# Graph attention's last row tiles: sums and bias on VectorE, a last step for what the keys don't need, and four buffers for the keys' halves

## The chip, the cores and the metric

The kernel runs on one core of one Trainium2 chip. The metric is the device time of one execution in microseconds; lower is better. Times are medians of several runs. A profile is one execution, with every instruction's start and length in a trace.

The engines are named as the profile names them: PE (TensorE's matmuls), PEld (its weight loads), DVE (VectorE), ACT (ScalarE), POOL (GpSimd) and SP, which only issues DMAs. A DMA can be issued on SP's or on POOL's queue; each engine and each queue works through its instructions in the order in which they stand there.

## What is computed

Two layers work on 2708 nodes with 512 features. Each normalizes its input, clears what is negative, and adds its result to its input. The first is a graph attention of eight heads; the second builds an attention of its own from the features and diffuses over it in two steps. Cut to what matters here:

```python
# layer 0: graph attention, H = 8 heads of D = 64
h = jnp.maximum(_layernorm(x, axis=-1), 0.0)
feats = jnp.einsum('nf,hfd->hnd', h, W)
dense = leaky_relu(e_self[:, :, None] + e_neigh[:, None, :]) + mask[None, :, :]
out = jnp.einsum('hnm,hmd->hnd', softmax(dense), feats) + b[:, None, :]
x = x + relu(out)                               # heads side by side
# layer 1: its input is the normalized, cleared x of layer 0
v = jnp.maximum(_layernorm(x, axis=-1), 0.0)
for s in range(2):
    Q, K = Xa @ W1, Xa @ W3                     # Xa starts as v
    A = nucleus_softmax(Q @ W2 @ K.T)           # keeps 0.9 of each row's mass
    Xf, Xb, Xa = Rf @ Xf, Rb @ Xb, A @ Xa
    Z = Z + (Xf @ U1[s] + Xb @ U2[s] + Xa @ U3[s])
x = x + layernorm(v + Z) * gamma + beta
```

## The kernel before

The nodes are cut into 22 row tiles, 21 of 128 rows and a last one of 20.

**The first layer** goes through six chunks of columns; the first four have four tiles, the last two three. The last chunk holds tiles 19, 20 and 21, which is 276 columns. For each chunk and each group of four heads a loop over all 22 tiles forms the attention's weights on DVE (L427) and multiplies them on PE (L429). ACT then copies the sums to `o_t` (L434). What turns a chunk's sums into finished rows is `finished`, for one tile at a time, in five steps:

- `turned`: loads the tile's x (`xt`) and transposes the sums on PE (L351).
- `shared`: the denominators and their reciprocal (L360, L362) and the sum for rows without neighbours (L365) on DVE; then on POOL the multiplication by the reciprocal (L367) and the bias of the attention (L368).
- `normed`: relu and the addition of x on DVE (L372); `moments`, which is two steps on DVE (L137, L138) and two on POOL (L139, L140); then on POOL the second layer's `beta` added into `xt` (L374) and its DMA to `xb_d` (L375).
- `cleared`: the normalization on DVE (L381), the clearing on ACT (L382), which gives `v`, and its DMA to `va_d` on POOL's queue (L383).
- `asked`: transposes v on PE (L389) and copies it on ACT (L391). `split_rows` splits v into a high and a low half: zeros into a ragged tile (L180, POOL), the high half (L181, DVE), the low half (L182, here on POOL) and a DMA of 512 KB to `vhl_d` (L183, POOL's queue). `project` forms keys and queries on PE (L160), takes them over on ACT (L165, L166), splits them on POOL (L170 to L172; L164 writes zeros first for the ragged tile) and sends them to `kq_d` (L173, POOL's queue).

In the first five chunks the steps of a finished chunk are spread over the next chunk's loop. For the last chunk (`final`) there is no such loop: `later` is filled by step, and each step is issued for the three tiles before the next step begins. The buffers of `split_rows` and `project` come from the pool `halves`, with one buffer per name. The order of the instructions on each engine in the first layer is made by a planner. It starts from the order of the code and from what is ready by its own estimate of times, and so it can differ from the code's order.

**The second layer** does two steps with the order on PE, ACT, DVE and SP fixed by the code. Its first instructions load the keys of all tiles from `kq_d` (L930: tiles 0 to 19 in a first pair of DMAs, tiles 20 and 21 in a second), then the queries (L509); then PE forms the logits of the first pair of tiles (L521), which ACT copies (L523) and DVE reduces (L548). `split_rows` and `project` are called there too, with pools of their own. `vhl_d` is read by L961, one row tile after the other, along with `s_d` (L963) for the diffusion's products on PE (L967); `va_d` by L937; `xb_d` at the end of the last step.

Of the kernel before, what the change touches and what calls it, by code (L numbers as in the profile page):

```python
# [9 lines left out]
F32 = mybir.dt.float32  # L10
# [14 lines left out]
P = 128  # L25
# [28 lines left out]
def kernel(  # L54
# [19 lines left out]
    nc = tc.nc  # L74
    N, D = x.shape
    H, _, DH = w_gat.shape
# [12 lines left out]
    TG = 4  # L89
# [42 lines left out]
    def moments(pool, src, pr):  # L132

        st = pool.tile([P, 6], F32, name="ln_st")
        mv = pool.tile([P, 2], F32, name="ln_mv")
        rs = pool.tile([P, 1], F32, name="ln_rs")
        nc.vector.bn_stats(st[:pr], src)  # L137
        nc.vector.bn_aggr(mv[:pr], st[:pr])  # L138
        nc.gpsimd.tensor_scalar(rs[:pr], mv[:pr, 1:2], LN_EPS, None, op0=OP.add)  # L139
        nc.gpsimd.tensor_tensor(rs[:pr], rs[:pr], nhalf[:pr], OP.pow)  # L140
        return mv[:pr, 0:1], rs[:pr]
# [10 lines left out]

    kw = const.tile([P, KD, 2 * DA], F32, name="kw")

    def project(pool, pk, v_t, t, s):


        pr = rows[t]
        for k in range(KD):
            nc.tensor.matmul(pk[:, :pr], lhsT=kw[:, k, :], rhs=v_t[:, k, :pr], start=(k == 0), stop=(k == KD - 1))  # L160
        big = pool.tile([P, P], F32, name="kq_b")
        hl = pool.tile([P, 2, P], F32, name="kq_hl")
        if pr < P:
            nc.gpsimd.memset(hl, 0.0)  # L164
        nc.scalar.copy(hl[:, 1, :pr], pk[:, :pr])  # L165
        nc.scalar.mul(big[:, :pr], pk[:, :pr], 4097.0)  # L166


        high, x = hl[:, 0, :pr], hl[:, 1, :pr]
        nc.gpsimd.tensor_tensor(high, big[:, :pr], x, op=OP.subtract)  # L170
        nc.gpsimd.tensor_tensor(high, big[:, :pr], high, op=OP.subtract)
        nc.gpsimd.tensor_tensor(x, x, high, op=OP.subtract)  # L172
        nc.gpsimd.dma_start(out=kq_d[s][:, :, t * P:(t + 1) * P], in_=hl)  # L173
# [28 lines left out]
    with ExitStack() as l0:  # L202
# [13 lines left out]
        with tc.tile_pool(name="l0w", bufs=1) as wp, tc.tile_pool(name="l0p", bufs=2) as pp, \  # L216
# [44 lines left out]
            for t in range(NT):  # L261
                pr = rows[t]
# [70 lines left out]
                            ap=[[0, P], [N, len(grp)], [1, cw]]))  # L333
            return r_b

        def finished(t, o_t, c0, bank):


            pr = rows[t]
            f3 = fsum.rearrange("p (h d) -> p h d", h=H)  # L340
            pns, held = [], []

            def turned():
                xt = work.tile([P, D], F32, name="xt0", bufs=3)
                nc.sync.dma_start(out=xt[:pr], in_=x[cols[t], :])
                held.append(xt)
                for g, grp in enumerate(hgroups):
                    pn = bank(g)
                    pns.append(pn[:, :HG * DV].rearrange("p (h d) -> p h d", h=HG))
                    for i, hd in enumerate(grp):  # L350
                        nc.tensor.transpose(pns[g][:pr, i, :], o_t[:, hd, c0:c0 + pr], ident[:DV, :DV])  # L351

            def shared():
                den = small.tile([P, H], F32, name="den")
                rden = small.tile([P, H], F32, name="rden")
                o = work.tile([P, D], F32, name="o", bufs=3)
                held.append(o)
                o3 = o.rearrange("p (h d) -> p h d", h=H)
                for pn, grp in zip(pns, hgroups):
                    nc.vector.tensor_scalar(den[:pr, grp[0]:grp[-1] + 1], pn[:pr, :, DH],  # L360
                                            lone_n[:pr, t:t + 1], None, op0=OP.add)
                nc.vector.reciprocal(rden[:pr], den[:pr])  # L362
                for pn, grp in zip(pns, hgroups):
                    s = slice(grp[0], grp[-1] + 1)
                    nc.vector.scalar_tensor_tensor(o3[:pr, s, :], f3[:pr, s, :], lone[:pr, t:t + 1],  # L365
                                                   pn[:pr, :, :DH], op0=OP.mult, op1=OP.add)
                nc.gpsimd.tensor_mul(o3[:pr], o3[:pr], rden[:pr].unsqueeze(2).to_broadcast([pr, H, DH]))  # L367
                nc.gpsimd.tensor_add(o[:pr], o[:pr], b_b[:pr])  # L368

            def normed():  # L370
                xt, o = held
                nc.vector.scalar_tensor_tensor(o[:pr], o[:pr], 0.0, xt[:pr], op0=OP.max, op1=OP.add)  # L372
                held.extend(moments(small, o[:pr], pr))
                nc.gpsimd.tensor_add(xt[:pr], o[:pr], beta_b[:pr])  # L374
                nc.gpsimd.dma_start(out=xb_d[cols[t], :], in_=xt[:pr])  # L375

            def cleared():
                _, o, mean, rs = held
                v = work.tile([P, D], F32, name="v", bufs=3)
                held.append(v)  # L380
                nc.vector.tensor_scalar(o[:pr], o[:pr], mean, rs, op0=OP.subtract, op1=OP.mult)  # L381
                nc.scalar.activation(v[:pr], o[:pr], AF.Relu)  # L382
                nc.gpsimd.dma_start(out=va_d[cols[t], :], in_=v[:pr])  # L383

            def asked():
                v = held[4]
                pt = bank(0).rearrange("p (k d) -> p k d", k=KD)
                for k in range(KD):
                    nc.tensor.transpose(pt[:, k, :pr], v[:pr, k * P:(k + 1) * P], ident[:pr, :pr])  # L389
                v_t = work.tile([P, KD, P], F32, name="v_t", bufs=2)  # L390
                nc.scalar.copy(v_t[:, :, :pr], pt[:, :, :pr])  # L391
                split_rows(halves, nc.gpsimd, v[:pr], t, vhl_d)
                project(halves, bank(1), v_t, t, 0)

            return [turned, shared, normed, cleared, asked]

        later = {}
        for ci, tiles in enumerate(tchunks):
            n0, n1 = tiles[0] * P, min((tiles[-1] + 1) * P, N)
            cw = n1 - n0  # L400
            r_bs = [shares(grp, n0, cw) for grp in hgroups[:1]]
            a_c = []
            for t in range(NT):
                pr = rows[t]
                a_c.append(adjp.tile([P, 512], F32, name="a_c", bufs=NT + 2))
                nc.sync.dma_start(out=a_c[t][:pr, :cw], in_=adj_t[cols[t], n0:n1])
                s_c = small.tile([P, 512], F32R, name="s_c", bufs=4)
                wide = len(tiles) * P
                if pr < P or cw < wide:
                    nc.gpsimd.memset(s_c.bitcast(F32), 0.0)  # L410
                nc.scalar.activation(s_c[:pr, :cw], a_c[t][:pr, :cw], AF.Copy,  # L411
                                     accum_out=cpart[:pr, t, ci:ci + 1])
                if t in tiles:
                    d = slice(t * P - n0, t * P - n0 + pr)
                    nc.gpsimd.tensor_tensor(s_c[:pr, d], s_c[:pr, d].bitcast(F32), ident[:pr, :pr], op=OP.add)
                nc.sync.dma_start(out=s_d[t * P:(t + 1) * P, n0:n0 + wide], in_=s_c[:, :wide].bitcast(F32))
            for t in tiles:
                row_sums(t)
            r_bs += [shares(grp, n0, cw) for grp in hgroups[1:]]
            o_t = work.tile([DV, H, 512], F32, name="o_t", bufs=1)  # L420
            for grp, r_b in zip(hgroups, r_bs):
                po = [ps_o.tile([P, 512], F32, name="po")[:DV] for _ in grp]
                for t in range(NT):
                    pr = rows[t]
                    for i, hd in enumerate(grp):
                        e = tp.tile([P, 512], F32, name="e")
                        nc.vector.scalar_tensor_tensor(e[:pr, :cw], r_b[:pr, i, :cw], kk[:pr, t, hd:hd + 1],  # L427
                                                       a_c[t][:pr, :cw], op0=OP.max, op1=OP.mult)
                        nc.tensor.matmul(po[i][:, :cw], lhsT=fw[:pr, t, hd, :], rhs=e[:pr, :cw],  # L429
                                         start=(t == 0), stop=(t == NT - 1))  # L430
                    for stage in later.pop(t, ()):
                        stage()
                for i, hd in enumerate(grp):
                    nc.scalar.copy(o_t[:, hd, :cw], po[i][:, :cw])  # L434

            final = ci == len(tchunks) - 1
            for i, t in enumerate(tiles):
                if final:
                    bank = lambda g: ps_o.tile([P, 512], F32, name="po")
                else:  # L440
                    bank = lambda g: ps_t.tile([P, 512], F32, name=f"pn{g}")
                for n, stage in enumerate(finished(t, o_t, t * P - n0, bank)):
                    later.setdefault(n if final else i * 5 + n, []).append(stage)
        for n in sorted(later):
            for stage in later[n]:
# [832 lines left out]
```

## Time and profile before

| | |
|---|---|
| median of three runs | 3710.2 us (3706.47 to 3715.27) |
| profiled execution, its own time | 3708.3 us |
| span of the profiled execution | 3706.5 us |
| busy, share of the span | PE 91%, DVE 70%, PEld 47%, ACT 42%, POOL 22% |
| TensorE's clock granted, mean | 0.966 |
| last matmul of the first layer's loop ends | 1052.4 us after the span's start |
| first matmul of the second layer starts | 1098.1 us |

A line of the timeline has the start and the length in us, the engine, the line of the code, the operation, the tile written and the tiles read, the shape, how many instructions were merged and, in brackets, how long the engine stood idle before it and what released it. A line of the waits has who waited, for what, the total in us, how often and the longest. The lines themselves stand in the prediction.

### The profile page before, as it was taken

How to read it: one execution, taken by the hardware profiler on the slowest of the kernel's cores; microseconds unless marked ns; L12 is line 12 of the kernel's file. 1: busy time of each engine (PE TensorE's matmuls, PEld its weight loads, DVE VectorE, ACT ScalarE, POOL GpSimd, SP SyncE). 2: the span in 40 equal slices, each digit the busy share in tenths (PEclk: the TensorE clock that was granted, in tenths of full speed). 3: DMA queues.
4: the chain of work that ended last, by engine and by line, in shares of the span. 5: the costliest groups of instructions: out<-in, count | busy, mean ns of one | idle time of the engine just before them, and what ended most of it. 6: DMA issues, size and time to landing. Idle time of an engine off the chain costs nothing. (4 is left out here: it accounts for less than half of the span.)

```text
span 3706.5 us, 35338 instructions
## 1 busy us (share of the span) xinstructions
PE 3367.4 (91%) x11143; PEld 1754.4 (47%) x11143; DVE 2612.9 (70%) x4820; ACT 1541.5 (42%) x2334; POOL 799.6 (22%) x1119
## 2 busy tenths in 40 slices
PE   7998999998966988989899899688999999999898
PEld 4433333333444545545455453445655565556452
DVE  4588888889957637365463651969988779777991
ACT  2343212111114674655666612345654556445511
POOL 4114140514331112121202121302112111121101
PEclk9999999999978999999999999999999999999999
DMA  3477424233228445454535353966556665566552
GB/s 113 152 252 243 137 80 150 80 105 103 74 87 278 164 157 187 145 183 149 205 131 196 128 191 100 302 203 225 175 187 208 233 216 204 183 213 234 201 201 66
DMA packets 276459, 634.08 MB, mean 171 GB/s; under 512 B 37210, under 2 KB 70442, under 8 KB 273244
## 3 DMA queue, kind: packets, MB, share of 16 engines
q1 hardware_dynamic: 249183, 540.99, 44.2%
q0 software_dynamic: 27024, 90.30, 6.3%
q8 instruction: 89, 1.46, 0.2%
q14 instruction: 163, 1.33, 0.1%
HBM read 509.07 MB, written 122.10 MB: 170 GB/s over the span
## 5 line engine op out<-in xcount | busy, mean ns | idle before, releaser
L1035 PE MATMUL a<-va,at 128*128 128x512 f32 (+2 forms) x1936 | 890.1, 599 | 14.0 <-ACT at L1020 13.5
L967 PE MATMUL q<-hl,s_r 128*128 128x512 f32 x2904 | 820.9, 429 | 62.5 <-DMA s_r<-s_d 62.2
L429 PE MATMUL po<-e,fw 128*65 128x512 f32 (+4 forms) x2112 | 838.7, 552 | 34.3 <-DVE e L427 21.8
L427 DVE SCALAR_TENSOR_TENSOR e<-r_b,kk,a_c 128x512 f32<-128x512 f32 (+4 forms) x1056 | 751.8, 741 | 73.5 <-PE po L429 23.7
L967 PEld LDWEIGHTS q<-hl,s_r 128*128 128x128 f32 x2904 | 544.4, 190 | 307.5 <-issue 133.2
L553 ACT ACTIVATE junk_a<-p,nth 128x2708 uint8<-128x2708 f32 (+1 forms) x240 | 613.1, 2554 | 70.6 <-POOL nth L572 66.8
L429 PEld LDWEIGHTS po<-e,fw 128*65 128x65 f32 (+1 forms) x2112 | 286.2, 140 | 546.7 <-issue 269.2
L1035 PEld LDWEIGHTS a<-va,at 128*128 128x128 f32 (+2 forms) x1936 | 337.1, 187 | 379.4 <-issue 342.7
L1076 PE MATMUL a<-u_k,v_t 128*128 128x512 f32 (+1 forms) x1056 | 489.9, 601 | 22.3 <-ACT xa L1043 15.4
L629 DVE SCALAR_TENSOR_TENSOR junk<-p,th 128x2708 bf16<-128x2708 f32 (+1 forms) x132 | 401.2, 3039 | 4.0
L1020 ACT COPY at<-t 128x512 f32<-128x512 f32 (+3 forms) x308 | 140.4, 477 | 494.5 <-PE t L1016 494.1
L1076 PEld LDWEIGHTS a<-u_k,v_t 128*128 128x128 f32 (+1 forms) x1056 | 188.9, 187 | 242.1 <-issue 182.9
L521 PE MATMUL t<-keys,q_t 128*128 128x452 f32 x528 | 167.1, 443 | 118.4 <-ACT p L523 98.1
L181 DVE TENSOR_SCALAR split_hl<-xe 128x512 int32<-128x512 int32 (+1 forms) x44 | 19.1, 434 | 257.1 <-ACT xe L977 210.7
L808 DVE MAX8 vn<-keep 128x8 f32<-128x2708 f32 (+1 forms) x66 | 196.8, 2981 | 2.3
L523 ACT COPY p<-t 128x452 f32<-128x452 f32 (+2 forms) x264 | 132.0, 538 | 126.5 <-PE t L521 82.3
L521 PEld LDWEIGHTS t<-keys,q_t 128*128 128x128 f32 x528 | 91.7, 211 | 189.2 <-ACT p L523 150.7
L411 ACT ACTIVATE s_c<-a_c 128x512 fp32r<-128x512 f32 (+3 forms) x132 | 76.1, 577 | 247.5 <-DMA a_c<-in_adj_t_dram 120.7
L1016 PE MATMUL t<-ident,keep 128*128 128x128 f32 (+1 forms) x968 | 147.2, 274 | 27.1 <-DVE keep L757 19.2
L1016 PEld LDWEIGHTS t<-ident,keep 128*128 128x128 f32 (+1 forms) x968 | 115.0, 139 | 107.5 <-issue 79.5
L548 DVE TENSOR_REDUCE nmx<-p 128x1 f32<-128x2708 f32 (+1 forms) x44 | 129.0, 2966 | 41.7 <-ACT p L523 41.7
L565 POOL TENSOR_TENSOR x<-sums,powers 128x4 f32<-128x4 f32 x22 | 44.7, 2033 | 508.7 <-ACT p L560 508.7
(296 smaller groups left out, 3151.9 us busy)
## 6 DMA issues: line engine op xcount, KB each, us to landing
s_r<-s_d SPq DMA_DIRECT2D x330, 256.0 KB
hl<-vhl_d SPq DMA_DIRECT2D x132, 512.0 KB
u_k<-in_L_gnn_U_dram SPq DMA_DIRECT2D x264, 256.0 KB
hl<-fhl_d SPq DMA_DIRECT2D x132, 512.0 KB
hl<-bhl_d SPq DMA_DIRECT2D x132, 512.0 KB
arow<-in_adj_dram SPq DMA_DIRECT2D x21, 1354.0 KB
s_d<-s_c SPq DMA_DIRECT2D x88, 256.0 KB
a_c<-in_adj_t_dram SPq DMA_DIRECT2D x84, 256.0 KB
```

The source lines that it names most:

```text
L427: nc.vector.scalar_tensor_tensor(e[:pr, :cw], r_b[:pr, i, :cw], kk[:pr, t, hd:hd + 1], a_c[t][:pr, :cw], op0=OP.max, op1=OP.mult)
L429: nc.tensor.matmul(po[i][:, :cw], lhsT=fw[:pr, t, hd, :], rhs=e[:pr, :cw], start=(t == 0), stop=(t == NT - 1))
L521: nc.tensor.matmul(pl[:, :c1 - c0], lhsT=q[:, i], rhs=self.keys[:, c0:c1], start=(i == 0), stop=(i == 1))
L523: nc.scalar.copy(p[:pr, c0:c1], pl[:pr, :c1 - c0])
L553: nc.scalar.activation(junk[:pr], self.p[i][:pr], func, **kw)
L629: v.scalar_tensor_tensor(junk_b[:pr], ps_[i][:pr], th, ps_[i][:pr], op0=OP.is_ge, op1=OP.mult, accum_out=dst)
L808: v.max(vs, keep[0][:pr])
L967: nc.tensor.matmul(half[j], lhsT=s_r[:, j * P:(j + 1) * P], rhs=hl[:, h], start=(c == 0 and h == 0), stop=(c == NT - 1 and h == 1))
L1016: nc.tensor.transpose(pt[:rows[c], j, :pr], keep[i][:pr, cols[c]], ident[:pr, :pr])
L1020: nc.scalar.copy(at[:r, j0:j1, :pr], pt[:r, j0:j1, :pr])
L1035: nc.tensor.matmul(pa[:pr], lhsT=at[:rows[c], j, :pr], rhs=va[:rows[c], c, :], start=(c == 0), stop=(c == NT - 1))
L1076: nc.tensor.matmul(pz[i][:rows[t]], lhsT=v_t[i][:, k, :rows[t]], rhs=u_k, start=(n == 0 and k == 0), stop=(n == 2 and k == KD - 1))
```

## The change

Four things change, all for the last chunk's three tiles, but for the number of buffers, which holds for every tile of the first layer.

- `finished` is told whether the chunk is the last one (`final`). If so, L367's multiplication and L368's addition are done by DVE instead of POOL.
- In `normed`, for the last chunk, DVE copies the rows o into `xt` before the moments; the addition of beta and its DMA (L374, L375) leave this step. They become `with_beta`, which then reads the copy.
- In `asked`, for the last chunk, `split_rows` is left out. A sixth step, `rest`, is issued after all others: `split_rows`, with the low half on DVE instead of POOL, and then `with_beta`.
- `project`'s two tiles, `kq_b` and `kq_hl`, get four buffers (`TG`) in the first layer instead of one. The second layer's calls are as before.

```diff
-    def project(pool, pk, v_t, t, s):
+    def project(pool, pk, v_t, t, s, bufs=None):
...
-        big = pool.tile([P, P], F32, name="kq_b")
-        hl = pool.tile([P, 2, P], F32, name="kq_hl")
+        big = pool.tile([P, P], F32, name="kq_b", bufs=bufs)
+        hl = pool.tile([P, 2, P], F32, name="kq_hl", bufs=bufs)
...
-                nc.gpsimd.tensor_mul(o3[:pr], o3[:pr], rden[:pr].unsqueeze(2).to_broadcast([pr, H, DH]))
-                nc.gpsimd.tensor_add(o[:pr], o[:pr], b_b[:pr])
+                eng = nc.vector if final else nc.gpsimd
+                eng.tensor_mul(o3[:pr], o3[:pr], rden[:pr].unsqueeze(2).to_broadcast([pr, H, DH]))
+                eng.tensor_add(o[:pr], o[:pr], b_b[:pr])
 
             def normed():
                 xt, o = held
                 nc.vector.scalar_tensor_tensor(o[:pr], o[:pr], 0.0, xt[:pr], op0=OP.max, op1=OP.add)
+                if final:
+                    nc.vector.tensor_copy(xt[:pr], o[:pr])
                 held.extend(moments(small, o[:pr], pr))
+                if not final:
+                    with_beta(o)
+
+            def with_beta(o):
+                xt = held[0]
                 nc.gpsimd.tensor_add(xt[:pr], o[:pr], beta_b[:pr])
                 nc.gpsimd.dma_start(out=xb_d[cols[t], :], in_=xt[:pr])
...
-                split_rows(halves, nc.gpsimd, v[:pr], t, vhl_d)
-                project(halves, bank(1), v_t, t, 0)
-
-            return [turned, shared, normed, cleared, asked]
+                if not final:
+                    split_rows(halves, nc.gpsimd, v[:pr], t, vhl_d)
+                project(halves, bank(1), v_t, t, 0, bufs=TG)
+
+            def rest():
+                split_rows(halves, nc.vector, held[4][:pr], t, vhl_d)
+                with_beta(held[0])
+
+            return [turned, shared, normed, cleared, asked] + [rest] * final
...
-                for n, stage in enumerate(finished(t, o_t, t * P - n0, bank)):
+                for n, stage in enumerate(finished(t, o_t, t * P - n0, bank, final)):
```

More of the change, by code (lines that the diff above doesn't have):

```diff
@@ L334, in shares, with finished @@
             return r_b
-        def finished(t, o_t, c0, bank):
+        def finished(t, o_t, c0, bank, final):
             pr = rows[t]
```

## The prediction

> **What bounds the kernel now.** I read the page first, then busy time by stretch around the end of the first layer, then the timeline, then the waits.
>
> ```profile
> PE 3367.4 (91%) x11143; PEld 1754.4 (47%) x11143; DVE 2612.9 (70%) x4820; ACT 1541.5 (42%) x2334; POOL 799.6 (22%) x1119
> ```
>
> TensorE is busy 91% of the span. The change touches none of its large groups, so it can only pay where TensorE stands still. The busy times (length, then PE, PEld, DVE, ACT, POOL, granted clock, DMA share, GB/s):
>
> ```profile
> 1000.00:1030.00 30.00, 30.00 (x128) 16.95 (x127) 30.00 (x71) 1.54 (x4) 1.79 (x4) 1.00 0.05 17
> 1060.00:1080.00 20.00, 8.56 (x36) 7.31 (x36) 9.12 (x18) 4.05 (x10) 18.64 (x26) 0.50 0.23 90
> 1080.00:1110.00 30.00, 11.29 (x38) 7.64 (x39) 5.72 (x3) 8.58 (x16) 5.98 (x11) 0.62 0.62 188
> ```
>
> Until 1052 PE and DVE are full. Then comes a hole of some 46 us: POOL is the busy engine in its first half (18.64 of 20), and hardly any engine works in its second. The timeline (start, length, engine, line; in brackets the idle time before) says what the hole consists of:
>
> ```profile
> 1052.88 0.22 DVE L360 TENSOR_SCALAR den<-po,lone_n 128x4 f32<-128x4 f32 x1 [4.69 <-PE po L351]
> 1056.62 1.51 DVE L372 SCALAR_TENSOR_TENSOR o<-o,xt 128x512 f32<-128x512 f32 x1 [0.34 <-POOL o L368]
> 1061.88 2.93 POOL L374 TENSOR_TENSOR xt<-o,beta_b 128x512 f32<-128x512 f32 x2
> 1065.38 0.25 POOL L139 TENSOR_SCALAR ln_rs<-ln_mv 128x1 f32<-128x1 f32 x1
> 1066.81 0.55 DVE L381 TENSOR_SCALAR o<-o,ln_mv,ln_rs 128x512 f32<-128x512 f32 x1 [2.41 <-POOL ln_rs L140]
> 1077.36 1.90 PE L160 MATMUL po<-v_t,kw 128*128 128x20 f32 x8 [0.37 <-ACT v_t L391]
> 1085.17 0.94 POOL L180 MEMSET split_hl<- 128x1024 f32 x1 [3.18 <-DMA vhl_d<-split_hl]
> 1088.14 0.31 POOL L164 MEMSET kq_hl<- 128x256 f32 x1 [2.03 <-DMA kq_d<-kq_hl]
> 1088.49 0.17 ACT L165 COPY kq_hl<-po 128x20 f32<-128x20 f32 x1 [9.16 <-POOL kq_hl L164]
> 1091.40 0.69 POOL L173 DMA_DIRECT2D kq_d<-kq_hl  x1 [0.29 <-POOL kq_hl L172]
> 1094.77 5.20 SPq L509 DMA_DIRECT2D q_t<-kq_d  x8
> 1098.13 5.01 PE L521 MATMUL t<-keys,q_t 128*128 128x452 f32 x12 [18.87 <-DMA q_t<-kq_d]
> ```
>
> Four things are to be seen. First, DVE's L372 takes 1.51 us here against a median of 0.679 in the chunks before: POOL's L367 runs beside it. Second, POOL does L374 of two tiles ahead of L139, though the code issues the moments first: the planner gives an idle engine whatever is ready, and L381 of tile 19 pays for it. Third, the last matmul of the keys (tile 21, L160) ends at 1079.26, but ACT takes its result at 1088.49 only. POOL had to write zeros into the two single buffers, which waited for the DMAs of tile 20. Fourth, the keys' DMA behind SP's queue waits for the last kq_d write, and L509 and everything of the second layer stand behind it. The waits agree:
>
> ```profile
> PE t L521 <- DMA q_t<-kq_d: 18.9, 1, 18.9
> ACT kq_hl L165 <- POOL kq_hl L164: 9.2, 1, 9.2
> ```
>
> **What the Trainium skill says.** "SBUF — State Buffer", section on the two separate sides: VectorE with two SBUF inputs and GpSimd share one pair of ports, and the loser is blocked for the whole instruction. The trace agrees: 1.51 against 0.679 us. "DMA: Bandwidth & Descriptors", section "Anatomy of one DMA": about 2.0 us plus bytes over 436 GB/s for a DMA issued on GpSimd. For the 128 KB of kq_d that makes 2.3 us (measured median 2.3), for the 512 KB of vhl_d 3.2 (measured 2.9 at the least). Same page, "SWDGE vs HWDGE vs iDMA": each DMA engine takes turns between its queues. In the trace tile 20's two writes take 6.2 and 6.8 us, since the 1.3 MB of keys issued from 1078.98 move beside them.
>
> **The change, part by part.**
>
> (1) Sums and bias on VectorE. POOL loses L367 and L368 of three tiles (1.03 to 1.59 us each). DVE gains six operations of 128x512 with two SBUF sources. The same form on DVE is L182 in the second layer, 0.692 us; neighbours overlap by about 0.07 (L137 starts 0.07 before L372 ends), so a step of 0.62 and 3.7 us in all. DVE's own share before is 1052.88 to 1056.29. With the six it ends at 1060.0.
>
> (2) The copy. One fp32 copy of 128x512 per tile, which no row shows. DVE's single-source rows of that size are L181 (0.42) and L381 (0.546): I take 0.5, on DVE's path. Per tile then L372 0.68, copy 0.50, L137 0.68, L138 0.17, less four overlaps: 1.75, three tiles 5.3, to 1065.3. The bias on the last step (L374) is ready as soon as the copy is, so I expect the planner to give it to an idle POOL again; one collision with L372 costs 0.83. L381 of tile 19 thus at 1066.1 instead of 1066.81: **0.7 us** won. Bounds: 1063.3 if the planner lets it in as soon as its L140 is done, 1067.5 with two collisions and some.
>
> (3) From there to the last L160 nothing is removed: L381, L382, L389, L391 and L160 of three tiles took 1066.81 to 1079.26, 12.45 us, with TensorE at clock 0.50. The same span gives 1078.6. Lower bound: the PE work alone (1.12+2.08+1.06+2.08+0.61+1.90 = 8.85) back to back, 2.4 us earlier.
>
> (4) Four buffers for the keys' halves. L164's zeros wait for nothing and go early; L165 no longer waits for a DMA. After L160, ACT needs 0.5 (tile 19: 1072.85 to 1073.32), and L170 to L172 at the pace of tile 21 (0.32 each) with 0.3 before the DMA 1.3: L173 at 1080.4 instead of 1091.40. In the other chunks these waits don't exist (POOL's L170 waits for ACT alone), so the buffers do nothing there.
>
> (5) What the keys don't need goes last: L180 to L183, L374 and L375 of three tiles, with L182 on DVE (3 x 0.692, behind L381 on DVE where nobody on the path waits). Each is queued on POOL with L173: L374 4.5, L375 1.9, L183 1.7, L180 0.94, together 9.0 us. The path's own POOL work after 1061 is 10.9 (L139 and L140 2.5, L383 1.8, L164 0.3, L170 to L172 4.2, L173 2.1). All 20 us fit just before 1081, so the cover is thin: I charge half an L374, 0.8 us, in front of tile 21's. L173 at 1081.2. A step that waits for a DMA's landing (L180, and L183 behind DVE's L181) is worse than a long one: its price is a rival below. The bound below is nothing, if the planner lets only ready work in.
>
> (6) From L173 to L521 it took 6.73 us (1091.40 to 1098.13): landing, the keys' second DMAs, q_t. Kept: L521 at 1087.9.
>
> Sum: 1098.1 - 1087.9 = **10.2 us**. Is it kept afterwards? The second layer starts from this point with all engines idle, and its first chain (L521, ACT's copies, DVE's maximum, the search) hangs on L521 alone. The deferred writes (1.5 MB of vhl_d, 0.55 MB of xb_d) can fall into a stretch with a DMA share of 0.97 (1110 to 1150), where 1 MB at its 332 GB/s is 3 us. But TensorE's fills there are through at 1181, and its next work waits 13.3 us for ACT, so 3 us vanish in that. vhl_d's last rows are read last, xb_d in the last step.
>
> The profiled execution took 3708.3 us (span 3706.5), which makes 3698.1; the median of the runs shown is 3710.2, 1.9 above, so a median of 3700.0 would fit as well.
>
> **The rivals.**
>
> *POOL's order spoils it.* L180 of tile 21 (and L183) is put ahead of tile 21's L170. vhl_d of tile 20 is issued near 1075 and lands near 1081 beside the keys; zeros, DVE's two steps and L183 reach to 1083.6; L173 at 1085, its write behind 512 KB of vhl_d (1.2 us more): L521 near 1094, 4 us won, **3704.3**. For it: the planner cannot know 6.2 us for a write. Against it: it ranks the last step last.
>
> *The keys' first DMA becomes late.* It waits for tile 19's kq_d, took 8 us (1078.98 to about 1087) and would be issued near 1076.5, landing at 1084.5. Two vhl_d writes beside it add 1.2 us each: 1086.9, still before 1087.9. With twice that contention, and q_t in turns with vhl_d, L521 falls at 1091: 7 us won, **3701.3**.
>
> *More is won.* The planner lets L381 in early, and PE runs its tiles back to back: 2 us from (2) or (3) and POOL free, **3695.3**.
>
> *Slower.* If the planner puts all of the last step ahead of tile 21's keys, POOL works off 1083.6 plus L374 and L375 of three tiles (6.4) to 1090.0, L173 falls at 1091.5, and its write queues behind 1.06 MB (2.4 us): L521 at 1100.7, **3710.8**. From L173 later than 1091.40 it is a loss. For it: L374 and L375 stood ahead of L139 before. Against it: tile 21's L170 is ready near 1079.
>
> That the change doesn't do what it says is part of the first rival: a last step in the code is only a lower rank for the planner.
>
> **How the numbers follow.** Chances: forecast 0.48, spoiled order 0.19, late keys 0.13, more won 0.13, slower 0.07. About 0.2% (7.4 us) is what a measurement of this kernel can tell from no change. Faster by more: the forecast and the "more won" case nearly whole (0.58 of 0.61), half of the late keys (0.06), a little of the spoiled order (0.02): 0.66. Slower by more: its case as priced falls short of that and needs a longer wait still, 0.04. Within: the rest, 0.30. The range runs from 3693.5 (more won, with the copy at its cheap end) to 3706.0 (spoiled order, carried to the median).
>
> **What would show it.** L367 and L368 on DVE at 0.69 us; L372 at 0.68, or 1.5 beside L374; L381 of tile 19 near 1066; no wait of L164 or L165 for a DMA; L173 of tile 21 near 1081 and L521 near 1088; the chain from L521 to the end as long as before. It is wrong if POOL waits for vhl_d ahead of tile 21's L170, if L521 waits for the keys' first DMA, or if the second layer is longer.

## The result, and the profile after

The change makes the kernel faster by about 0.15%: the ratio to the kernel before is 0.9985, with a 95% interval of 0.9978 to 0.9992. The medians are 3704.18 us after and 3711.23 us before, of 19 runs each; single runs of either kernel lie up to 12 us apart. The ratio stands for 5.6 us (3.0 to 8.2) where 10.2 were forecast: the time lies inside the stated range, but the forecast gain lies outside the interval.

Lines from L365 on have moved: L367 and L368 are L368 and L369 now, L374 and L375 are L382 and L383, L381 is L389, L382 is L390, L389 and L391 are L397 and L399, L930 is L943, L509 is L522, L521 is L534. Below, each number of a line is that of the kernel spoken of.

Busy time by stretch, of the changed kernel (the columns are as in the prediction):

```profile
1060.00:1080.00 20.00, 8.56 (x36) 7.30 (x36) 9.80 (x22) 4.33 (x12) 16.63 (x29) 0.50 0.35 111
1080.00:1110.00 30.00, 15.92 (x56) 10.56 (x56) 7.04 (x4) 14.72 (x21) 2.25 (x4) 0.73 0.75 238
```

PE does 15.92 us of work between 1080 and 1110, where it was 11.29: the second layer starts sooner. POOL is still the busy engine of the first half (16.63 against 18.64). The timeline of the changed kernel shows where the hole got shorter and where it didn't:

```profile
1058.98 2.01 POOL L382 TENSOR_TENSOR xt<-xt,beta_b 128x512 f32<-128x512 f32 x1 [58.13 <-DVE xt L375]
1064.07 0.81 DVE L389 TENSOR_SCALAR o<-o,ln_mv,ln_rs 128x512 f32<-128x512 f32 x1
1067.58 0.55 DVE L389 TENSOR_SCALAR o<-o,ln_mv,ln_rs 128x512 f32<-128x512 f32 x1 [2.62 <-POOL ln_rs L140]
1068.75 0.57 ACT L399 COPY v_t<-po 128x512 f32<-128x512 f32 x1
1076.02 1.90 PE L160 MATMUL po<-v_t,kw 128*128 128x20 f32 x8 [0.37 <-ACT v_t L399]
1076.56 11.63 SPq L943 DMA_DIRECT2D keys<-kq_d  x4
1076.74 0.57 POOL L183 DMA_DIRECT2D vhl_d<-split_hl  x1
1077.99 0.17 ACT L165 COPY kq_hl<-po 128x20 f32<-128x20 f32 x1 [2.03 <-PE po L160]
1080.36 0.69 POOL L173 DMA_DIRECT2D kq_d<-kq_hl  x1 [0.29 <-POOL kq_hl L172]
1088.24 6.13 SPq L522 DMA_DIRECT2D q_t<-kq_d  x8
1091.91 4.89 PE L534 MATMUL t<-keys,q_t 128*128 128x452 f32 x12 [14.00 <-DMA q_t<-kq_d]
```

ACT takes the last keys (L165) as soon as PE has them, at 1077.99; before, it waited 9.16 us for a memset. The last kq_d is issued at 1080.36 instead of 1091.40. But the queries' loads (L522) follow it only 7.9 us later, where it had been 3.4. The first layer's loop ended 1.4 us sooner in this execution than in that of before (the last L351 starts at 1051.00 and 1052.38). Such a shift comes without any change of the first layer: e5 below, whose first layer is that of before, has this point at 1050.19. So I measure **the hole**, from the start of that L351 to the first matmul of the second layer: 45.7 us before, 40.9 after.

What became longer is the landing of the last writes. The answers for the tile kq_d around the hole end with the times from issue to landing (least, median, most) of the last three tiles' writes, before:

```profile
DMA to landing us min/median/max: 2.2/2.3/6.8
```

and after:

```profile
DMA to landing us min/median/max: 2.5/6.7/8.1
```

By tile these are 2.3, 6.8, 2.2 before and 2.5, 8.1, 6.7 after. Before, one write of the three was slow, and not the last one; now the last two are.

### The profile page after: what moved, and what is told of

It reads as the page before. It is cut to its first block, busy times and chain, and to the rows that moved or that the text cites. A ratio compares the mean times of both kernels' runs of the same rounds, so it can differ in the third digit from the quotient of the medians.

```text
span 3703.3 us, 35350 instructions
## 1 busy us (share of the span) xinstructions
PE 3377.6 (91%) x11143; PEld 1759.4 (48%) x11143; DVE 2617.2 (71%) x4832; ACT 1541.2 (42%) x2334; POOL 799.5 (22%) x1110
## 5 line engine op out<-in xcount | busy, mean ns | idle before, releaser
L1048 PE MATMUL a<-va,at 128*128 128x512 f32 (+2 forms) x1936 | 890.0, 599 | 14.4 <-ACT at L1033 14.1
L534 PE MATMUL t<-keys,q_t 128*128 128x452 f32 x528 | 167.4, 445 | 113.9 <-ACT p L536 98.4
L534 PEld LDWEIGHTS t<-keys,q_t 128*128 128x128 f32 x528 | 91.9, 211 | 184.9 <-ACT p L536 151.5
```

Source lines behind the costliest of these rows:

```text
L534: nc.tensor.matmul(pl[:, :c1 - c0], lhsT=q[:, i], rhs=self.keys[:, c0:c1], start=(i == 0), stop=(i == 1))
L1048: nc.tensor.matmul(pa[:pr], lhsT=at[:rows[c], j, :pr], rhs=va[:rows[c], c, :], start=(c == 0), stop=(c == NT - 1))
```

## The experiments

All ratios are to the kernel before, with a 95% interval; 0.001 is 3.7 us. Holes and landings come from one profiled execution of each kernel.

| kernel | hole, us | ratio | in us |
|---|---|---|---|
| before | 45.7 | 1 | 0 |
| the change | 40.9 | 0.9985 (0.9978 to 0.9992) | -5.6 |
| e1, buffers alone | 41.8 | 0.9989 (0.9982 to 0.9996) | -4.1 |
| e2, sums alone | 45.6 | 0.9996 (0.9988 to 1.0005) | -1.5 |
| e3, all but the buffers | 43.2 | 0.9995 (0.9988 to 1.0002) | -1.9 |
| e4, the change, keys cut at tile 19 | 37.6 | 0.9981 (0.9975 to 0.9988) | -7.0 |
| e5, before, keys cut at tile 19 | 46.3 | 0.9995 (0.9989 to 1.0002) | -1.9 |
| e6, the change, last step behind L173 | 44.0 | 0.9988 (0.9981 to 0.9995) | -4.5 |
| e7, e4 and e6 | 43.8 | 0.9997 (0.9988 to 1.0005) | -1.1 |
| e8, e7 and ramps first | 43.2 | 0.9998 (0.9990 to 1.0006) | -0.7 |
| e9, e4 and ramps first | 38.8 | 0.9983 (0.9977 to 0.9990) | -6.3 |
| e10, the change and ramps first | 41.5 | 0.9977 (0.9970 to 0.9984) | -8.5 |
| e11, the change, two buffers each | 43.0 | 0.9991 (0.9985 to 0.9998) | -3.3 |
| e12, e11 and keys cut at tile 19 | 40.1 | 0.9984 (0.9976 to 0.9992) | -5.9 |

**Which part does it.** e1 is the kernel before with `project(..., bufs=TG)` alone.

> The kernel before with only the four buffers for the keys' halves. The measure is the hole from the start of the last L351 to the first matmul of the second layer: 45.7 us before, 40.9 with the whole change. My theory: the buffers free tile 21's keys from the DMAs of tile 20, so L173 of tile 21 falls near 31 us after L351 instead of 39, but its write then lands 7 us later beside the 1.3 MB of keys, so the hole is 42 and the time 3 to 4 us under before. If the landing took 2.4 us as the prediction had it, the hole would be 37.5. If the buffers were not what counts, 45.5.

The hole is 41.8, as the theory has it: L173 of tile 21 starts 30.3 us after L351, and its write takes 6.8 us. The buffers alone bring 3.9 of the 4.8 us. Put in last, they bring less: from e3 below, with everything but them, to the change it is 2.3 us. The parts overlap, so no one share belongs to the buffers.

e2 is the kernel before with `eng = nc.vector if final else nc.gpsimd` for the two operations alone.

> The kernel before with only the sums and the bias of the last three tiles on VectorE. Theory: the first L381 comes 2 us earlier, tile 20's DMAs 2 us earlier, and the waits of the single buffers stay as they are: hole 43.5, time 2 us under before. Rival (POOL is covered by the wait for tile 20's DMAs, and that wait depends on nothing that moves): hole 45.7, no change.

The rival's number was right, and my theory missed: hole 45.6. The first normalization (L381 in the kernel before, L382 here) does come sooner, 11.7 us after L351 instead of 14.4. Of these 2.7 us, 0.8 are left when tile 20's keys are sent (L173 at 28.1 instead of 28.9). That write then takes 7.4 us instead of 6.8, and L164 of tile 21, which waits for it, starts at 35.6 instead of 35.8. ACT waits for L164:

```profile
ACT kq_hl L165 <- POOL kq_hl L164: 10.1, 1, 10.1
```

It was 9.2 in the kernel before: ACT was done with tile 20 sooner and stands idle for longer. The matmuls of tile 21's keys themselves come no sooner (the last L160 ends at 27.1 instead of 26.9).

e3 is the changed kernel with `project(halves, bank(1), v_t, t, 0)` again.

> The changed kernel with one buffer for the keys' halves again. Theory: L164 waits for tile 20's write to kq_d once more, and in POOL's order it stands behind L180, which waits for tile 20's vhl_d; L173 of tile 21 falls near 36 us after L351, when the keys' first DMA is through, so it lands in 2.5 us: hole 43, that is 2 us above the changed kernel. If the last step alone carried the gain: hole 41.

Hole 43.2, as expected, though L180 waits for nothing here, other than I thought: tile 20's vhl_d is issued before the keys' load starts and lands in 3.2 us. Sums and last step together bring 2.5 us without the buffers. About half of it comes before L164 of tile 21 (34.5 us after L351 instead of 35.8), the other half between L164 and L173 (1.9 us instead of 3.3), where tile 21's split no longer stands. From e1 to the change, sums and last step bring 0.9 us of the hole, all of it between the end of the last L160 (27.0 and 26.9 us after L351) and L173 (30.3 and 29.4). So the sums bring nothing beside the buffers either, as far as these traces tell; no run leaves out the sums alone.

**Why the last write lands late.** Two explanations: the keys' first load (1.3 MB, issued when tile 19's keys have landed) moves on the same 16 DMA engines, or tile 20's 512 KB of vhl_d stand ahead in POOL's own queue. In the changed kernel's busy times, the stretch at and after the last L173 has hardly any engine at work, and the DMA engines full (the last three columns are granted clock, DMA share and GB/s):

```profile
1080.00:1084.00 4.00, 0.00 (x0) 0.00 (x0) 0.00 (x0) 0.00 (x0) 0.75 (x2) 0.50 1.02 303
```

e4 takes most of the keys' load out of the way:

```diff
-            h = (NT - NT % G - G) * P
+            h = (NT - NT % G - G) * P if last else tchunks[-1][0] * P
```

> The changed kernel with the second layer's first loads of the keys cut at tile 19 instead of tile 20, so that 1.25 MB of keys wait for nothing of the last three tiles and move before their writes. Theory (the engines' turns between the keys' load and the write of tile 21 make it land late): L173 to landing 2.4 us instead of 7, hole 36.2 us, time 4.7 us under the changed kernel. Rival (512 KB of vhl_d ahead of it in POOL's own queue): hole 40, time unchanged. A third: the keys' memory is still taken by the first layer, so that the load cannot start before: hole 41.

The load starts at 1070.4 instead of 1076.6, and the write of tile 21 lands in 2.5 us. It is tile 19's that takes 6.9 now. The line of e4:

```profile
DMA to landing us min/median/max: 2.5/3.8/6.9
```

Tile 21's write tells against the queue as the cause by itself: it has tile 20's 512 KB, which land 1.6 us after its issue, ahead of it and loses 0.3 us. Tile 19's tells less, since two writes stand ahead of it: its 512 KB land 1.5 us after its issue, tile 21's 40 KB of va_d 4.6 us after it.

The other half is in e3, where a write of keys meets the load with its queue empty. Its timeline and the answer for kq_d:

```profile
1074.53 0.55 POOL L183 DMA_DIRECT2D vhl_d<-split_hl  x1 [0.81 <-DVE split_hl L182]
1075.39 14.61 SPq L943 DMA_DIRECT2D keys<-kq_d  x4
1077.63 0.69 POOL L173 DMA_DIRECT2D kq_d<-kq_hl  x1 [0.29 <-POOL kq_hl L172]
...
DMA to landing us min/median/max: 2.2/2.2/7.0
```

Tile 20's 512 KB (L183) take 3.2 us and land at 1077.73, 0.1 us after tile 20's keys are sent (L173). These keys are the ones that take 7.0 us, with nothing left ahead of them. So the load alone makes a write late, and without the load 512 KB ahead in the queue cost 0.3 us.

In e4 the hole is 37.6 us, 3.3 less, of 4.7 expected; the time is 7.0 us under before. Against the change itself the intervals overlap.

e5 is the same edit on the kernel before.

> The kernel before with the keys' first loads cut at tile 19 and nothing else. Theory (the keys' 1.3 MB slow the writes beside them): tile 20's writes land in 3.0 and 2.4 us instead of 6.2 and 6.8, the two memsets on POOL start 3 to 4 us earlier, hole 42 instead of 45.7, time 3 to 4 us under before. Rival (POOL's own queue makes the writes late): hole 45, time unchanged.

A miss: hole 46.3. Tile 20's writes do land in 2.9 and 2.2 us. But the load now starts at 1071.3, right beside tile 19's two writes, which take 7.4 and 7.5 us; with one buffer, ACT's L165 of tile 20 waits for the second of them. From the answer for kq_d in e5:

```profile
  ACT kq_hl L165: 6.8, 1
...
DMA to landing us min/median/max: 2.2/2.2/7.5
```

The slow landing follows the load, as my theory of it says; that a single buffer hands it on to the next tile I had not thought of.

e6 is the changed kernel with the last step queued behind the last write of keys, as an order on POOL alone:

```diff
-                split_rows(halves, nc.vector, held[4][:pr], t, vhl_d)
-                with_beta(held[0])
+                with tc.issue_after(sent[-1].ins):      # the last L173
+                    split_rows(halves, nc.vector, held[4][:pr], t, vhl_d)
+                    with_beta(held[0])
```

> The changed kernel with the whole last step queued on POOL behind the last tile's L173, so that neither vhl_d nor xb_d of the last tiles stands ahead of a write of keys. Theory (the keys' load makes the landing late): L173 of tile 21 comes 1 us earlier, its write still lands late, in 5 us or more, hole 39 to 40, time 1 to 2 us under the changed kernel, some of it given back as 1.5 MB of vhl_d then move beside the queries' loads. Rival (vhl_d ahead of it in POOL's queue): landing 2.4 us, hole 35.5.

Neither. All three writes land in 2.2 us, and L173 of tile 21 starts 26.0 us after L351 instead of 29.4. Yet the hole is 44.0. The timeline of e6 says why:

```profile
1078.56 0.69 POOL L173 DMA_DIRECT2D kq_d<-kq_hl  x1 [0.29 <-POOL kq_hl L172]
1082.37 0.43 DVE L181 TENSOR_SCALAR split_hl<-v 128x512 int32<-128x512 int32 x1 [14.08 <-DMA vhl_d<-split_hl]
1085.83 0.32 DVE L505 TENSOR_SCALAR below_d<-across,down 128x128 bf16<-128x128 f32 x1
1086.28 2.57 SPq L945 DMA_DIRECT2D keys<-kq_d  x4
1096.58 1.85 PE L536 MATMUL t<-keys,q_t 128*128 128x452 f32 x4 [19.59 <-DMA q_t<-kq_d]
```

The keys' load starts at 1086.28, though all it reads has landed by 1081. It waits for DVE's `below_d`, which stands on DVE behind tile 20's split, which waits for tile 19's vhl_d. The keys' memory is memory that the first layer, and the small pool of ramps behind it, give back. As the load came after the writes here, e6 doesn't tell the two explanations apart by itself.

e7 is e4 and e6 together.

> The changed kernel with both: keys' loads cut at tile 19, last step behind the last L173. Theory and rival agree on the landing, 2.4 us: hole 35.5, time 5 to 6 us under the changed kernel and 12 under before. If it isn't under the kernel that only cuts the loads (hole 36.2 expected), the writes put off to the end slow the queries' loads by what they gave up before.

Hole 43.8 and no gain that could be told from none: the same wait for `below_d` (82.2 us in the list of waits, counted from SP's last work).

e8 and e9 are e7 and e4 with the four operations of the ramps moved ahead of the first layer; e10 is the changed kernel with that move.

> The kernel with keys cut at tile 19 and the last step behind the last L173, and besides the four ramp operations (ones, across, down, below_d), which use nothing of the first layer, moved ahead of it. Without that move the keys' first load started at 33.7 us after L351, just after below_d on DVE, which stood behind tile 20's split waiting for a DMA. Theory (that operation alone holds the keys' memory): the load starts by 20 us after L351, L173 of tile 21 stays at 26, its write lands in 2.2 us, hole 33 to 35 us against 45.7 before, time 11 us under before. Rival (the memory is also held by tiles that the last step reads): the load still starts after 30 us, hole 43, time 1 to 2 us under before.

> The changed kernel with keys cut at tile 19 and the ramp operations moved ahead of the first layer, the last step left where it is. Theory (below_d held the keys' load until 20.1 us after L351): the load starts some us sooner and meets fewer of the writes; the write of tile 21 landed in 2.5 us already, so the hole falls by 1 us at most, to 36.5 to 37.6, and the time is as without the move, 8 us under before. If other tiles hold the memory: no difference at all.

> The changed kernel with the ramp operations moved ahead of the first layer and nothing else. Theory (here the keys' first load waits for tile 19's write, not for below_d, which is done 6 us before): hole 40.9 us as in the changed kernel, no difference beyond 0.5 us in the hole, time 5 to 7 us under before. A second measurement of the changed kernel's time.

In e8 the rival was right. The timeline of e8:

```profile
1076.88 1.27 POOL L392 TENSOR_TENSOR xt<-xt,beta_b 20x512 f32<-20x512 f32 x1
1078.17 2.40 SPq L946 DMA_DIRECT2D keys<-kq_d  x4
1080.62 16.90 SPq L525 DMA_DIRECT2D q_t<-kq_d  x8
```

The keys' load starts as POOL ends the addition of beta to the last tile, which is part of the last step. It reads nothing of that, so the wait is for memory that keys and `xt` share. Then the queries' loads take 16.90 us on SP's queue: two are issued at once, the third only at 1093.79, when the last vhl_d has landed (11.7 us of waits for vhl_d in all), and the loads of hl stand behind them. The hole doesn't show this, as it ends with the first tile's logits. e9 missed its hole by 1 to 2 us: the load starts 16.0 us after L351, again as POOL ends that addition, and then meets tile 19's vhl_d, which takes 7.3 us. Tile 20's L183, which waits for it by way of DVE, stands on POOL ahead of the last keys. e10's hole is 41.5, 0.6 above that of the change where 0.5 at most was expected. Its time, 8.5 us under before, is more than the hole explains: in all three kernels with the ramps first, DVE forms the first attention weights some 3 us sooner (at 136.8 to 137.4 us after the span's start, against 139.3 to 140.9 in the others). That was not what I moved them for. The traces show where it begins: with the ramps first, the planner puts the first loads of x ahead of the loads of `b_b` and `beta_b` on SP's queue (issued at 0.73 instead of 1.64 us in e10 and the change), and DVE's first moments start at 3.4 instead of 7.6 to 7.8 us. The first line is the change's, the second e10's:

```profile
7.68 0.69 DVE L137 BATCH_NORM_STATS2 ln_st<-xt 128x6 f32<-128x512 f32 x1 [6.40 <-DMA xt<-in_x_dram]
3.38 0.69 DVE L137 BATCH_NORM_STATS2 ln_st<-xt 128x6 f32<-128x512 f32 x1 [1.66 <-DMA xt<-in_x_dram]
```

No run moves these loads alone.

e11 gives the halves of v two buffers and those of the keys two instead of four; in POOL's order vhl_d of tiles 20 and 21 then stand ahead of the last kq_d. e12 cuts the keys' loads at tile 19 besides.

> The changed kernel with two buffers for the halves of v and two, not four, for those of the keys, so that no step of the last one waits for the DMA just before it; on POOL, vhl_d of tiles 20 and 21 then stands ahead of the last kq_d. Theory (the keys' 1.3 MB make the last write late): landing 7 us as before, hole 41, and as the queries' loads no longer wait for the last vhl_d, the first load of hl comes 1 us sooner after the logits; time as the changed kernel or 1 us less. Rival (data ahead of it in POOL's own queue makes it late): with 1 MB ahead instead of 0.5 the landing takes 8.5 us or more, hole 43.

> The same with the keys' loads cut at tile 19. Theory: the last write lands in 2.5 to 4 us, hole 37 to 38.5, time 7 to 9 us under before. Rival: the 1 MB of vhl_d ahead of it keeps the landing at 5 us or more, hole 40 or more, time as the changed kernel.

In e11 the last landing is 7.6 us, between the two, and the hole is the rival's; 1.4 us of that come from L173 starting later behind the added L183. The first load of hl comes 2.3 us after the first logits, in the change 2.5, so of the 1 us expected there little is seen. e12's hole, 40.1, is the rival's number as well but not for the rival's reason: with two buffers, L164 of tile 21 waits for tile 19's write, which takes 5.7 us. It lands 0.1 us after tile 20's vhl_d, which stands ahead of it and takes 9.6 us beside the earlier load. The last write is issued only at 1082.46, when both vhl_d have just landed, so its 2.2 us exclude nothing. From e12:

```profile
1080.57 0.31 POOL L164 MEMSET kq_hl<- 128x256 f32 x1 [2.43 <-DMA kq_d<-kq_hl]
1082.46 0.68 POOL L173 DMA_DIRECT2D kq_d<-kq_hl  x1 [0.29 <-POOL kq_hl L172]
```

No version is shown to beat the change: e4 and e10 have the lowest ratios, and their intervals overlap with its own.

## Why the prediction was right, and where it was not

The direction, the place and the part were right: the buffers release the last keys, the second layer starts sooner. By the prediction's own steps, in us after the last L351:

| point | before | forecast | after |
|---|---|---|---|
| L381 of tile 19 starts | 14.4 | 13.7 | 13.1 |
| last L160 ends | 26.9 | 26.2 | 26.9 |
| L173 of tile 21 starts | 39.0 | 28.8 | 29.4 |
| first matmul of the second layer | 45.7 | 35.5 | 40.9 |

- **(1) and (2), sums and copy.** The durations held: 0.67 to 0.69 us for each operation on DVE, 0.41 for the copy where I took 0.5. As forecast, the planner puts L382 on POOL as soon as the copy is done, and L373 (L372 before) collides with it once (1.51 us). L389 of tile 19 comes 1.4 us sooner. But the 0.7 us forecast to reach the end of L160 did not: it is lost by tile 20. Its L140 stands on POOL behind L382 and L383 of tile 20 and L382 of tile 21, so its L389 starts at 1067.58, and ACT clears tile 20's rows before it copies tile 19's transposed ones (L399 at 1068.75, 2.0 us after PE had them). Step (3), "nothing is removed", thus cost 13.9 us instead of 12.45. e2 shows the same: a first tile sooner, the hole unchanged.
- **(4) and (5), buffers and last step.** From the end of L160 to L173: 12.1 before, 2.6 forecast, 2.4 after. This is where the gain is. The last step's cover held as well: L183 of tile 20 stands in the middle of tile 20's three steps, and no wait for a DMA stands ahead of tile 21's keys. One sum under (5) is off: L170 to L172 add up to 3.4 us in the trace of before, not 4.2. The charge of 0.8 us beside it was not worked out from that sum.
- **(6) is the step that failed.** I kept the 6.73 us from L173 to the first logits; it took 11.55. I had read that the keys' load and tile 20's writes slow each other, and then carried over a landing of 2.2 us from a moment when that load was done. Moving the write 9.7 us forward moved it into the load: 4.8 us of the 10.2 are given back there, 4.5 of them in the landing (6.7 us instead of 2.2). I held this for a rival (the keys' first load late, 7 us won), with the wrong end of it: it is not the load that ends last but the write beside it. e4 shows the landing at 2.5 us once the load is elsewhere, with 512 KB still ahead in POOL's queue, and e3 shows 7.0 us beside the load with nothing ahead. The trace of before had the price already: tile 20's write landed at 1088.1, 9.1 us after the load's issue. In the runs the 15 writes of keys that were issued 1.8 to 6.8 us after the load landed 9.1 to 11.1 us after the load's issue, so within that span it counted when the load went, not when the write did.
- **POOL's queue in (6).** It can have a part all the same: beside the load the writes land in the order of their issue, tile 20's vhl_d at 1084.5, the two kq_d at 1086.9 and 1087.1, so what stands ahead, slowed itself, passes its wait on. How much of the 4.8 us goes that way the runs don't separate (e11's landing, 0.9 us later with twice as much ahead, fits some). The Trainium skill ("DMA: Bandwidth & Descriptors", section "SWDGE vs HWDGE vs iDMA") says that each DMA engine takes turns between the two kinds of queue; the runs put a price to it, 2.2 us turned to 6.7 to 8.1 in the change. In the changed kernel both queues move packets between 1081 and 1086; in e3 the turns don't show: from 1078 to 1082 only SP's queue moves packets, and the write's move after that.
- **The gain after the hole.** That it is kept is borne out within what the runs can tell: for the change, e1 to e5, e7, e11 and e12, the ratio and the change of the hole differ by 2.5 us at most, and the intervals reach about as far; e6's time gains 2.8 us more than its hole. In e8 and e9 it is lost in part: with the shorter first layer they should stand near 6 and 10 us under before, and stand 0.7 and 6.3 under. In e8, SP's queue held up by the last vhl_d may be the cause; no run tests it, and e6, with 6.8 us of such waits, loses nothing. In e9 it stays open. In the changed kernel that wait is 0.7 us.
- **Range and chances.** The time fell into the range because the range reached to the rival with 4 us won, not because the sum held: there was luck in that. The chance of 0.66 for more than 0.2% was too high: it gave the late keys 0.13, and the gain, 0.15%, stayed under that 0.2%.

## What to carry to other kernels

When a step on a chain of waits is moved, price the waits behind it at the place where they will be, not where they were: a small write that is issued beside a large load lands when the load lets it. A buffer that is freed, and an operation that is put off, both decide when memory comes back; where the next stage's tiles lie in that memory, putting work off can hold up the very loads that it was to make room for. And when one of several waits in a row is shortened, look for what ended second: in e2 the sums came sooner, but POOL's work for the next tile and the wait for a buffer ended where they had.

## What the runs showed of the hardware

- A write of 128 KB issued on POOL's queue landed in 2.2 to 2.6 us when it was issued ahead of the keys' load or 9 us or more after it, and in 6.5 to 8.2 us when it was issued 1.8 to 4.2 us after this load of 1.3 MB on SP's queue (nine kernels). One of 512 KB landed in 2.9 to 3.6 us when it was issued 0.7 us or more ahead of the load or 9 us or more after it, and in 6.2 to 9.6 when it was issued from 0.1 us before to 3.4 us after it.
- In the three kernels where the first loads of x stood ahead of those of `b_b` and `beta_b` on SP's queue, DVE had x 4.2 to 4.4 us sooner (3.4 us after the start instead of 7.6 to 7.8), and the first loop began some 3 us sooner.
